# Roots and inverse roots of small tiles: powers on GpSimd in place of ScalarE's root, a Newton step and reciprocals

## The chip, the core and the metric

The kernel runs on one core of one Trainium2 chip. The time is the device time of one execution in microseconds (us). The median of three runs before the change is 863.87 us (863.44 to 865.81). The profile was taken in an execution of 861.47 us, whose span is 859.7 us with a mean granted TensorE clock of 0.921.

The engines are named as in the profile: PE is TensorE (matmuls), PEld its weight load, DVE is VectorE, ACT is ScalarE, POOL is GpSimd, SP only issues transfers.

## What is computed

Four graph layers run on x (3327 nodes, 64 features) and a dense 0/1 adjacency matrix (3327 x 3327). Each layer adds its result to x, and each begins with a layer norm and a relu:

```python
m = mean(x); v = var(x)
h = maximum((x - m) / sqrt(v + eps), 0)
x = x + layer(h, adj, ...)
```

- Layers 0 and 3 are hyperbolic: a weight sigmoid(left_i + right_j) * adj_ij for each pair of nodes, a logarithmic map of node j seen from node i, the weighted sum over j, an exponential map and a projection onto the ball. Norms of rows enter them through `sqrt(sum(x*x))`, tanh and artanh.
- Layer 1 weights the last neighbours of a row by powers of a half ("decay").
- Layer 2 is a GRU pair fed by signed sums over neighbours and a signed attention.

So square roots and inverse roots occur once per node at a few places: in the four norms as 1/sqrt(v + eps), at the start of layers 0 and 3 as the root of the squared norm, and at their ends in the length of the step and in the projection.

## The kernel before

The nodes are padded to 26 tiles of 128, so a quantity with one value a node is a tile of 128 partitions by 26 elements, and X is 128 x 26 x 64. `HALVES` cuts the 26 tiles into two times 13, and much of the work on X is done in two such halves, so that ScalarE and VectorE can work behind one another.

`sqrt_` (L94) takes a small tile and gives its root: ScalarE computes Sqrt (L98), then VectorE does one Newton step, s = (s + x/s)/2, in four instructions: reciprocal (L99), product (L100), sum (L101), half (L102). Where the inverse is wanted, a fifth instruction (L126, L697, L416) takes the reciprocal.

`norm_relu` (L111) runs at the start of each layer: sums (L117), difference (L120), squares on ScalarE (L121), sums of squares (L123), v + eps (L124), then the root, the reciprocal (L126), and max(h, 0) * sd (L128).

`hyperbolic_series` (L308) is layer 0 (r is None) and layer 3. In its setup, x2 (squared norms, L368) gives ia2 (L375), Xr (L379) and the two half-precision parts hi (L380, on ScalarE) and lo (L384); TensorE transposes them (L391), ScalarE and VectorE copy the transposes out to XT and XE (L393, L395), and small matmuls (L401) give the left and right terms. The root of max(x2, 1) (L381, L382) is copied to `root` (L414) and enters z (L416 to L418), by which the terms are multiplied (L422, L428). The main loop then goes over 104 pairs of a column chunk and a row tile: sigmoid on ScalarE (L504), times adjacency on GpSimd (L512), matmuls (L519, L520), a square on ScalarE (L526), two products on VectorE (L530, L531), accumulating matmuls (L537, L545). Its end (L603 on) is a long file of small instructions on 128 x 26 tiles: L639 to L703, with the root of v2 in layer 3 (L656), Tanh (L646 or L658), the root of n2 (L696) and its reciprocal (L697); then the update of X (L710, L711).

`plain_decay` (L1201) is layer 1: masks on VectorE (L1258), counting matmuls (L1265), Exp on ScalarE (L1271), accumulating matmuls (L1282). Its norm is called at L1303. `plain_gat` (L1345) is layer 2: its norm is at L1367, then the sums over neighbours (L1378), reciprocals of the degrees (L1395 to L1397) on VectorE, and the GRU (L1408 on). `ball` (L278) prepares constants of a hyperbolic layer; for layer 3 it takes the root of one value a partition (L302). `gru_weights` (L1180) loads small weights through GpSimd's DMA queue (L1184 to L1196) and adds biases on GpSimd (L1197).

ScalarE holds one table of functions at a time. Sqrt, Exp, and Sigmoid with Tanh need different tables; a load (ACT_TABLE_LOAD) is put by the compiler ahead of an activation that isn't in the loaded table. `table_of` (L105) runs an activation on one element only to have a load happen early.

What sets the order: outside the main loops each engine's instructions are put in order by a planner of the framework, by data dependencies and its own estimate of when operands are ready; instructions of later program text can come early. Inside `tc.manual_schedule` (the main loop of the hyperbolic layers, L442; most of `plain_decay`, L1242) the order on ScalarE, VectorE, TensorE and GpSimd is that of the program text. Each engine works through its queue in order, and an instruction that waits holds up all behind it. In `plain_decay`, GpSimd also adds a bias to all of X (L1333), written at step 4 of the loop.

Of the kernel before, what the change touches and what calls it, by code (L numbers as in the profile page):

```python
# [9 lines left out]
F32 = mybir.dt.float32  # L10
# [3 lines left out]
AF = mybir.ActivationFunctionType  # L14
OP = mybir.AluOpType
# [4 lines left out]
P = 128  # L20
T = 26
# [25 lines left out]
def tile_gnn4(ctx: ExitStack, tc: tile.TileContext, x, adjT, att0, b0, w1, bias1, w_gat, a_gat,  # L47
# [4 lines left out]
    V, G, A, PE = nc.vector, nc.gpsimd, nc.scalar, nc.tensor  # L52

    const = ctx.enter_context(tc.tile_pool(name="const", bufs=1))
# [8 lines left out]
    def column(value, name):  # L63
        t = const.tile([P, 1], F32, name=name)
        V.memset(t, value)
        return t

    one_c = column(1.0, "one_c")
    tiny_c = column(1e-19, "tiny_c")
    spare = const.tile([P, 1], F32, name="spare")  # L70
    nodes = const.tile([P, T], F32, name="nodes")
    V.memset(nodes, 1.0)
# [21 lines left out]
    def sqrt_(pool, src, name):  # L94

        s0 = pool.tile(list(src.shape), F32, name=name)
        rc = pool.tile(list(src.shape), F32, name=name + "_r")
        A.activation(s0, src, AF.Sqrt)  # L98
        V.reciprocal(rc, s0)  # L99
        V.tensor_mul(rc, rc, src)  # L100
        V.tensor_add(s0, s0, rc)  # L101
        V.tensor_scalar(s0, s0, 0.5, None, op0=OP.mult)  # L102
        return s0

    def table_of(f, after=None):  # L105

        A.activation(spare, one_c if after is None else after, f)
# [3 lines left out]
    def norm_relu(pool, h, dst=None):  # L111

        s = pool.tile([P, T], F32, name="ln_s")
        v = pool.tile([P, T], F32, name="ln_v")
        sq = pool.tile([P, T, D], F32, name="ln_sq")
        for ts in HALVES:
            V.reduce_sum(s[:, ts], X[:, ts, :], axis=AX.X)  # L117
        V.tensor_scalar(s, s, 1.0 / D, None, op0=OP.mult)
        for ts in HALVES:
            V.tensor_sub(h[:, ts, :], X[:, ts, :], wide(s[:, ts]))  # L120
            A.activation(sq[:, ts, :], h[:, ts, :], AF.Square)  # L121
        for ts in HALVES:
            V.reduce_sum(v[:, ts], sq[:, ts, :], axis=AX.X)  # L123
        V.tensor_scalar(v, v, 1.0 / D, LN_EPS, op0=OP.mult, op1=OP.add)  # L124
        sd = sqrt_(pool, v, "ln_sd")
        V.reciprocal(sd, sd)  # L126
        for o, ts in enumerate(HALVES):
            V.scalar_tensor_tensor(h[:, ts, :] if dst is None else dst[:, o], h[:, ts, :], 0.0, wide(sd[:, ts]),  # L128
                                   op0=OP.max, op1=OP.mult)
# [148 lines left out]
    def ball(att, b_att, r, min_norm, min_norm2, after=None):  # L278

        k = "0" if r is None else "1"  # L280
        wc = const.tile([P, 2], F32, name="wc" + k)
        with nc.allow_non_contiguous_dma(reason="128 weights"):
            for o in range(2):
                nc.scalar.dma_start(wc[o * D:(o + 1) * D, :],
                                    bass.AP(tensor=att.tensor, offset=att.offset, ap=[[1, D], [D, 2], [1, 1]]))
        wlr = const.tile([P, 2, 3], BF, name="wlr" + k)
        for i in range(3):
            G.tensor_copy(wlr[:, :, i], wc)
            if i < 2:
                G.tensor_tensor(wc, wc, wlr[:, :, i], op=OP.subtract)  # L290
        bcol = const.tile([P, 1], F32, name="bcol" + k)
        nc.scalar.dma_start(bcol, bcast_rows(b_att))
        cc, sqc, isqc, um, maxn2 = [const.tile([P, 1], F32, name=n + k) for n in ("cc", "sqc", "isqc", "um", "maxn")]
        if r is None:
            for t, value in ((cc, 1.0), (sqc, 1.0), (isqc, 1.0), (um, 0.0), (maxn2, min_norm2)):
                V.memset(t, value)
        else:
            nc.scalar.dma_start(cc, bcast_rows(r))
            V.scalar_tensor_tensor(cc, after, -3e38, cc, op0=OP.min, op1=OP.max)
            V.tensor_mul(cc, cc, cc)  # L300
            V.reciprocal(cc, cc)
            V.tensor_copy(sqc, sqrt_(const, cc, "sq"))  # L302
            V.reciprocal(isqc, sqc)
            V.tensor_scalar(um, sqc, min_norm / MIN_NORM, None, op0=OP.mult)
            V.tensor_scalar(maxn2, cc, min_norm2, None, op0=OP.mult)
        return wlr, bcol, cc, sqc, isqc, um, maxn2

    def hyperbolic_series(r, params, ok, masks=None, done=None):  # L308
# [17 lines left out]
        with ExitStack() as st:  # L326
# [14 lines left out]
            root = pers.tile([P, T], F32, name="root")  # L341
            wlr, bcol, cc, sqc, isqc, um, maxn2 = params

            with tc.tile_pool(name="hsp", bufs=1) as tp, tc.tile_pool(name="hsps", bufs=2, space=PSUM) as ps:
                A.memzero(X0)
                Xe = tp.tile([P, T, KE], F16, name="Xe")
                E = Xe[:, :, D:]
# [13 lines left out]

                H = tp.tile([P, T, D], F32, name="H")
                norm_relu(tp, H)
                sq = tp.tile([P, T, D], F32, name="sq")
                for ts in HALVES:
                    A.activation(sq[:, ts, :], H[:, ts, :], AF.Square)
                for ts in HALVES:
# [3 lines left out]
                ax = tp.tile([P, T], F32, name="ax")  # L371
# [6 lines left out]
                for ts in HALVES:  # L378
                    V.tensor_mul(Xr[:, ts, :], H[:, ts, :], wide(ia2[:, ts]))  # L379
                    A.activation(hi[:, ts, :], Xr[:, ts, :], AF.Copy, scale=SX)  # L380
                V.tensor_scalar(root, x2, 1.0, None, op0=OP.max)  # L381
                root_ = sqrt_(tp, root, "zs")  # L382
                for ts in HALVES:
                    V.scalar_tensor_tensor(lo[:, ts, :], Xr[:, ts, :], SX, hi[:, ts, :], op0=OP.mult, op1=OP.subtract)  # L384

# [25 lines left out]
                    V.tensor_copy(E[:, :, k:k + src.shape[-1]], src)  # L411


                V.tensor_copy(root, root_)  # L414
                z = tp.tile([P, T], F32, name="z")
                V.reciprocal(z, root)  # L416
                V.tensor_mul(z, z, ax)
                V.tensor_scalar(z, z, 0.5 * ARTANH_CLIP / SX, isqc, op0=OP.mult, op1=OP.mult)  # L418
                lr = tp.tile([P, T, 2], F32, name="lr")
                V.reduce_sum(lr, pw[:, :6 * T].rearrange("p (t k i) -> p t k i", k=2, i=3), axis=AX.X)  # L420
                left = tp.tile([P, T], F32, name="left")
                V.tensor_mul(left, lr[:, :, 0], z)  # L422
                pl = parts3(left, "pl", BF)
                table_of(AF.Sigmoid, root[:, :1])
                pe = ps.tile([P, 4 * P], F32, name="pe", bufs=1)
                PE.matmul(pe[:3 * T, :P], pl.rearrange("p t k -> p (t k)"), ident_bf, start=True, stop=True)
                A.activation(LT, pe[:3 * T, :P], AF.Copy)
# [175 lines left out]
            with tc.tile_pool(name="hse", bufs=1) as tp:  # L603
# [30 lines left out]
                t = new("t")  # L634
                if r is None:


                    f = MIN_NORM
                    p2 = new("p2")  # L639
                    V.tensor_scalar(p2, v2, f * f, None, op0=OP.mult)  # L640
                    by, g = new("by"), new("g")
                    V.tensor_scalar(by, p2, -1.0, 1.0, op0=OP.mult, op1=OP.add)
                    V.tensor_scalar(g, by, MIN_NORM, None, op0=OP.max)
                    V.reciprocal(g, g)
                    V.tensor_mul(t, root, g)
                    A.activation(th, t, AF.Tanh)  # L646
                    V.reciprocal(t, t)
                    V.tensor_mul(th, th, t)
                    V.tensor_mul(th, th, g)
                    y2 = mul("y2", th, th)  # L650
                    V.tensor_mul(y2, y2, x2)
                    V.scalar_tensor_tensor(vh, vh, f, th, op0=OP.mult, op1=OP.mult)
                else:

                    V.tensor_scalar(t, v2, 1e-8, None, op0=OP.max)
                    t = sqrt_(tp, t, "ts")  # L656
                    V.tensor_scalar(t, t, um, None, op0=OP.max)
                    A.activation(th, t, AF.Tanh)  # L658
                    V.reciprocal(t, t)
                    V.tensor_mul(th, th, t)  # L660
                    y2 = mul("y2", th, th)
                    V.tensor_mul(y2, y2, v2)
                    V.tensor_mul(vh, vh, th)
                    p2 = x2
# [23 lines left out]
                n2 = mul("n2", ah, x2)  # L688
# [4 lines left out]
                V.tensor_mul(mm, mm, am)  # L693
                V.tensor_add(n2, n2, mm)
                V.tensor_scalar(n2, n2, maxn2, None, op0=OP.max)
                n2 = sqrt_(tp, n2, "ns")  # L696
                V.reciprocal(n2, n2)  # L697
                V.tensor_scalar(n2, n2, 1.0 - 0.004, 1.0, op0=OP.mult, op1=OP.min)
                V.tensor_scalar(n2, n2, isqc, None, op0=OP.mult)
                V.tensor_mul(ah, ah, n2)  # L700
# [14 lines left out]
    def hyperbolic(att, b_att, r, min_norm, min_norm2):  # L715
# [7 lines left out]
        with ExitStack() as st:  # L723
# [17 lines left out]
            with tc.tile_pool(name="hyp", bufs=1) as tp, tc.tile_pool(name="hyps", bufs=2, space=PSUM) as ps:  # L741
# [8 lines left out]

                H = tp.tile([P, T, D], F32, name="H")
                norm_relu(tp, H)
                sq = tp.tile([P, T, D], F32, name="sq")
# [447 lines left out]
    def plain_decay(masks, zo, deg):  # L1201
# [10 lines left out]
        with ExitStack() as st:  # L1212
# [29 lines left out]
            with tc.tile_pool(name="pdacc", bufs=1, space=PSUM) as pa, tc.manual_schedule(  # L1242
# [57 lines left out]
                make_mask(1)  # L1300
                with tc.tile_pool(name="pdp", bufs=1) as tp:
                    H = tp.tile([P, T, D], F32, name="H")
                    norm_relu(tp, H)  # L1303
                    table_of(AF.Exp)
                    parts = split2(pers, H, "h2")
                for o in range(2):
                    cnt[o] = pa.tile([P, 2, 512], F32, name=f"cnt{o}")
                for k in range(K_ + 2):
# [29 lines left out]
                    if k - 2 >= T:  # L1338
                        b = steps[k - 2][1]
                        drop_diagonal(masks[b // 2][:, b % 2, :], b, 0, NP)  # L1340
                table_of(AF.Sqrt)
            with tc.tile_pool(name="pdps", bufs=2, space=PSUM) as ps:
                from_pairs(ps, outP, add, wt, range(6, T // 2))

# [195 lines left out]
```

## Time and profile before

The table gives times of the timeline, in us from the span's start.

| stage | stretch |
|---|---|
| layer 0: norm and setup | 5.3 to 33.3 |
| layer 0: main loop | 33.3 to 283.6 |
| layer 0: end | 283.6 to 304.9 |
| layer 1: norm | 304.9 to 320.2 |
| layer 1: loop | 320.2 to 447 |
| layer 2: end of layer 1, norm | 447 to 478.7 |
| layer 2: sums, then GRU | 478.7 to 560 |
| layer 3: norm and setup | 560 to 588 |
| layer 3: main loop | 588 to 831 |
| layer 3: end, store | 831 to 859.7 |

A line of the timeline gives start, duration, engine, line of the kernel, operation, what is written and read, shapes, and in brackets how long the engine had been idle before and what ended that. Several instructions of one line can stand in one row (x2). VectorE overlaps the start of an instruction with the end of the one before when there is no dependency between them, so starts can lie closer together than durations.

In the profile ACT_TABLE_LOAD occurs 12 times, each of 1283 ns: five at L98, four at L107 (inside `table_of`), one each at L345, L658 and L1426. The small Sqrt activations at L98 are ten: four in norms, two in setups, two for n2, one for the step's length in layer 3, one for the constant of one value a partition. Each takes 203 to 226 ns.

### The profile page before, as it was taken

The numbers are of one execution on the slowest core, as the hardware profiler recorded it, in microseconds if no ns is written. First come the engines' busy times: TensorE is split into PE (matmuls) and PEld (weight loads), VectorE is DVE, ScalarE is ACT, GpSimd is POOL, SyncE is SP. The second block draws the span as 40 slices with busy tenths as digits, with TensorE's granted clock in tenths as the row PEclk, the third lists the DMA queues.
The fourth block names the chain that finished last, engine by engine and source line by source line (L and its number), as shares of the span: only waits on it lengthen the run. The fifth ranks groups of instructions, "written<-read, shape, count | busy, mean of one in ns | idle before, by whom it ended". The sixth has DMA issues, their size and how long they took to land.

```text
span 859.7 us, 11940 instructions
## 1 busy us (share of the span) xinstructions
PE 672.2 (78%) x4264; PEld 245.2 (29%) x4264; DVE 728.3 (85%) x1020; ACT 577.1 (67%) x712; POOL 425.7 (50%) x309
## 2 busy tenths in 40 slices
PE   0489998989989219989990997617999899899960
PEld 0312232323322004434440562212222233232220
DVE  7389888889889899998989946795998889888976
ACT  3578878888978237777770306457888789788751
POOL 3289997998989410003110000005777677676730
PEclk9789999999999759999995899957999999999995
DMA  2556666666665428998944530001000000000001
GB/s 41 139 173 194 190 180 172 184 186 184 185 179 148 170 83 302 358 364 308 360 166 169 195 127 1 0 0 23 1 1 10 1 1 10 1 1 1 1 2 43
DMA packets 53877, 104.27 MB, mean 121 GB/s; under 512 B 8016, under 2 KB 30064, under 8 KB 53808
## 3 DMA queue, kind: packets, MB, share of 16 engines
q1 hardware_dynamic: 48704, 103.10, 37.8%
q10 hardware_dynamic: 4656, 0.08, 0.3%
q8 instruction: 35, 0.57, 0.3%
q14 instruction: 34, 0.28, 0.1%
q0 software_dynamic: 448, 0.24, 0.1%
HBM read 100.85 MB, written 0.85 MB: 118 GB/s over the span
## 4 chain that ended last, share of the span: by engine, by line
PE 46%; DVE 35%; ACT 11%; issue 4%; DMA 2%; ACTq 1%; DVEq 0%; SPq 0%; POOL 0%; POOLq 0%
DVE sig L531 11%; DVE L L530 10%; PE cnt L1265 9%; PE acc L537 7%; PE L L519 6%; PE acc L545 6%; ACT y L526 6%; PE acc L1282 5%; PE L L520 5%; PE acc L1378 4%; ACT sig L504 2%; DMA XC<-XT 1%; DVE deg L1397 1%; DVE X L711 1%; PE pt L391 1%
## 5 line engine op out<-in xcount | busy, mean ns | idle before, releaser
L512 POOL TENSOR_TENSOR sig<-mask,sig 128x768 f32<-128x768 fp8e4 (+1 forms) x104 | 174.5, 1679 | 215.7 <-DMA XC<-XT 153.4
L530 DVE SCALAR_TENSOR_TENSOR L<-y,L 128x768 f32<-128x768 f32 (+1 forms) x208 | 213.3, 1025 | 50.0 <-ACT y L526 48.0
L526 ACT ACTIVATE y<-L,shift_c 128x768 f32<-128x768 f32 (+1 forms) x208 | 198.1, 953 | 81.6 <-PE L L520 80.8
L531 DVE TENSOR_TENSOR sig<-L,sig 128x768 f32<-128x768 f32 (+1 forms) x208 | 213.2, 1025 | 21.7
L512 POOL TENSOR_TENSOR sig<-adj,sig 128x768 f32<-128x768 f32 (+1 forms) x104 | 202.6, 1960 | 27.5 <-ACT sig L504 22.4
L504 ACT ACTIVATE sig<-leftB,right 128x768 f32<-128x768 f32 (+1 forms) x208 | 203.7, 980 | 0.0
L537 PE MATMUL acc<-sig,Xr 128*64 128x384 f32 (+1 forms) x832 | 193.0, 542 | 2.1 <-DVE sig L531 2.1
L519 PE MATMUL L<-XC,XT 128*128 128x384 f16 (+1 forms) x416 | 146.5, 352 | 37.8 <-DVE sig L531 27.9
L520 PE MATMUL L<-XF,XE 73*128 73x384 f16 (+1 forms) x416 | 144.7, 348 | 0.0
L1271 ACT ACTIVATE w<-cnt,ebias 128x832 bf16<-128x832 f32 x104 | 93.7, 950 | 30.5 <-PE cnt L1265 30.5
L1178 DVE TENSOR_SCALAR_CACHE_REDUCE same<-adj 128x1664 bf16<-128x1664 f32 x52 | 97.7, 1879 | 3.1 <-DMA adj<-in 3.0
L519 PEld LDWEIGHTS <-XT 128*128 128x128 f16 x416 | 41.1, 99 | 198.1 <-DVE sig L531 154.7
L545 PE MATMUL acc<-sig,X 128*32 128x384 f32 (+1 forms) x832 | 94.2, 525 | 0.0
L1265 PE MATMUL cnt<-mask,after 128*128 128x416 fp8e4 x208 | 54.9, 347 | 23.3 <-DVE mask L1258 20.7
L178 POOL TENSOR_TENSOR mask<-mask,offdiag 128x128 fp8e4<-128x128 fp8e4 x26 | 13.4, 535 | 107.5 <-PE cnt L1265 105.5
L1265 PE MATMUL cnt<-mask,rest 128*128 128x416 fp8e4 x208 | 54.8, 346 | 12.4 <-ACT w L1271 12.4
L537 PEld LDWEIGHTS acc<-sig,Xr 128*64 128x64 f32 x832 | 41.3, 135 | 70.2 <-issue 63.9
L1258 DVE TENSOR_SCALAR mask<-adj 128x1664 fp8e4<-128x1664 f32 x52 | 53.3, 1033 | 1.4 <-DMA adj<-in 1.2
L1282 PE MATMUL acc<-w,h 128*64 128x416 bf16 x416 | 47.1, 349 | 0.0
L520 PEld LDWEIGHTS <-XE 73*128 73x128 f16 x416 | 41.5, 100 | 18.2 <-issue 2.2
L391 PE MATMUL pt<-ident_h,Xp 128*128 128x128 f16 x52 | 5.9, 313 | 41.5 <-DVE Xp L384 41.5
L1378 PE MATMUL acc<-mask,h 128*64 128x416 fp8e4 x416 | 37.9, 344 | 0.3
(295 smaller groups left out, 567.7 us busy)
## 6 DMA issues: line engine op xcount, KB each, us to landing
adj<-in SPq DMA_DIRECT2D x65, 832.0 KB, 6.4
adj<-in SPq DMA_DIRECT2D x78, 384.0 KB, 3.8
adj<-in SPq DMA_DIRECT2D x26, 512.0 KB, 4.7
XC<-XT SPq DMA_DIRECT2D x12, 96.0 KB, 2.6
X<-in SPq DMA_DIRECT2D x1, 832.0 KB, 4.5
out<-X SPq DMA_DIRECT2D x2, 416.0 KB, 2.7
XC<-XT SPq DMA_DIRECT2D x4, 128.0 KB, 5.1
gw<-in POOLq DMA_DIRECT2D x4, 48.0 KB, 6.4
```

Of the source, the lines that this page charges most:

```text
L504: A.activation(sig, leftB[c], AF.Sigmoid, bias=right[:, b:b + 1])
L512: G.tensor_tensor(sig, adj, sig, op=OP.mult)
L519: PE.matmul(L[:, o, :], XT[:, rows], XC[c][:, o, :], start=True, stop=False)
L520: PE.matmul(L[:, o, :], XE[:, rows], XF[c][:, o, :], start=False, stop=True)
L526: A.activation(ys[k], Ls[k], AF.Square, scale=-0.5 / SX ** 2, bias=shift_c)
L530: V.scalar_tensor_tensor(L, y, G3, L, op0=OP.add, op1=OP.mult)
L531: V.tensor_mul(sig, L, sig)
L537: PE.matmul(acc[c][0][o * D:(o + 1) * D, :n], Xr[:, b, :], sigs[k][:, o, :], start=b == 0, stop=b == T - 1)
L545: PE.matmul(acc[c][1][q:q + 32, :n], X0[:, b - 1 + i, :], w[:, o, :], start=b == 1, stop=b == T - 1, tile_position=(0, q))
L1178: V.tensor_scalar(same, adj, 0.0, 0.0, op0=OP.is_equal, op1=OP.add, accum_out=count)
L1265: PE.matmul(cnt[o][:, h, :BK], w, cols(k, o, h), start=w is after and steps[k][1] == T - 1, stop=True, skip_group_check=True)
L1271: A.activation(ws[k][:, o, :, :], cnt[o][:, :, :BK], AF.Exp, scale=-LN2, bias=ebias)
```

## The change

Every call of `sqrt_` on these paths is replaced by GpSimd's `tensor_tensor` with the operation `pow`, whose second operand is a constant 128 x 26 tile filled with 0.5 or -0.5. The inverse root comes out directly, so Newton step and reciprocal go. In the setup of the hyperbolic layers two powers are taken, one for the root (needed at the layer's end) and one for its inverse (needed for z). With Sqrt gone, ScalarE needs only the tables with Sigmoid and Tanh, and with Exp: the calls of `table_of` are moved or changed to match. The aim is to take table loads, hand-overs and small VectorE instructions out of the file of dependent steps, and to use an engine that is idle there.

```diff
@@ -67,6 +67,10 @@
     tiny_c = column(1e-19, "tiny_c")
+    exponents = {}
+    for value in (0.5, -0.5):
+        exponents[value] = const.tile([P, T], F32, name=f"e{len(exponents)}")
+        V.memset(exponents[value], value)
@@ -122,8 +126,8 @@   (norm_relu)
         V.tensor_scalar(v, v, 1.0 / D, LN_EPS, op0=OP.mult, op1=OP.add)
-        sd = sqrt_(pool, v, "ln_sd")
-        V.reciprocal(sd, sd)
+        sd = pool.tile([P, T], F32, name="ln_sd")
+        G.tensor_tensor(sd, v, exponents[-0.5], op=OP.pow)
@@ -299,7 +303,7 @@   (ball)
-            V.tensor_copy(sqc, sqrt_(const, cc, "sq"))
+            G.tensor_tensor(sqc, cc, exponents[0.5][:, :1], op=OP.pow)
@@ -342,6 +346,7 @@   (hyperbolic_series, setup)
+                table_of(AF.Sigmoid)
                 A.memzero(X0)
...
                 V.tensor_scalar(root, x2, 1.0, None, op0=OP.max)
-                root_ = sqrt_(tp, root, "zs")
+                zr = tp.tile([P, T], F32, name="zr")
+                G.tensor_tensor(zr, root, exponents[-0.5], op=OP.pow)
+                G.tensor_tensor(root, root, exponents[0.5], op=OP.pow)
...
-                V.tensor_copy(root, root_)
                 z = tp.tile([P, T], F32, name="z")
-                V.reciprocal(z, root)
-                V.tensor_mul(z, z, ax)
+                V.tensor_mul(z, zr, ax)
...
-                table_of(AF.Sigmoid, root[:, :1])
@@ -653,7 +657,7 @@   (end of layer 3)
                     V.tensor_scalar(t, v2, 1e-8, None, op0=OP.max)
-                    t = sqrt_(tp, t, "ts")
+                    G.tensor_tensor(t, t, exponents[0.5], op=OP.pow)
@@ -693,8 +697,7 @@   (end of layers 0 and 3)
                 V.tensor_scalar(n2, n2, maxn2, None, op0=OP.max)
-                n2 = sqrt_(tp, n2, "ns")
-                V.reciprocal(n2, n2)
+                G.tensor_tensor(n2, n2, exponents[-0.5], op=OP.pow)
@@ -1300,8 +1303,8 @@   (plain_decay)
+                    table_of(AF.Exp)
                     norm_relu(tp, H)
-                    table_of(AF.Exp)
...
-                table_of(AF.Sqrt)
+                table_of(AF.Sigmoid)
```

## The prediction

> **What bounds the kernel now.** I read the engines' shares first, then busy time by stage, then the chain of work that ended last, then the timeline around each root.
>
> ```profile
> PE 672.2 (78%) x4264; PEld 245.2 (29%) x4264; DVE 728.3 (85%) x1020; ACT 577.1 (67%) x712; POOL 425.7 (50%) x309
> ```
>
> No engine is full over the whole span, since the stages differ. Busy time by stage (columns: stretch, length, then PE, PEld, DVE, ACT and POOL busy with counts, granted clock, DMA share, GB/s) shows where the roots lie:
>
> ```profile
> 5.30:33.30 28.00, 8.12 (x95) 7.33 (x95) 22.28 (x65) 17.41 (x26) 5.99 (x17) 0.96 0.09 11
> 33.30:283.60 250.30, 226.10 (x1300) 67.03 (x1304) 213.09 (x220) 197.42 (x233) 217.85 (x136) 0.97 0.64 180
> ...
> 304.90:320.20 15.30, 1.57 (x5) 0.61 (x6) 14.68 (x19) 6.22 (x9) 3.70 (x1) 0.50 0.33 111
> ...
> 447.00:478.70 31.70, 8.00 (x50) 4.76 (x46) 30.44 (x38) 9.19 (x14) 0.00 (x0) 0.62 0.36 135
> ```
>
> In the second row, a big loop, four engines are busy, and the change touches nothing there. In the other three, and in the starts and ends like them (about 150 us together), TensorE is nearly idle and a single file of VectorE instructions, with a few ScalarE steps in it, sets the time. All roots but one lie in such files, so the latency from the operand to the finished root goes into the end one to one. The last root of the kernel, in the timeline:
>
> ```profile
> 835.83 0.18 DVE L655 TENSOR_SCALAR t<-v 128x26 f32<-128x26 f32 x1
> 836.23 1.28 ACT L98 ACT_TABLE_LOAD   x1 [2.80 <-issue]
> 837.52 0.23 ACT L98 ACTIVATE ts<-t 128x26 f32<-128x26 f32 x1
> 837.76 1.28 ACT L658 ACT_TABLE_LOAD   x1
> 837.78 0.32 DVE L99 RECIPROCAL ts_r<-ts 128x26 f32<-128x26 f32 x1 [1.77 <-ACT ts L98]
> ...
> 838.79 0.24 DVE L657 TENSOR_SCALAR ts<-ts,um 128x26 f32<-128x26 f32 x1
> ```
>
> From the operand at 836.01 to its use at 838.79 is 2.78 us: a table load that is waited for, the root, a Newton step in four VectorE instructions. Where the table is already loaded, root, Newton step and reciprocal take about 1.65 us. Next, the root in the norm ahead of the decay stage, which shows something else:
>
> ```profile
> 310.95 1.96 DVE L123 TENSOR_REDUCE ln_v<-ln_sq 128x13 f32<-128x832 f32 x2
> 311.00 3.70 POOL L1333 TENSOR_TENSOR X<-X,bias 128x1664 f32<-128x1664 f32 x1 [8.01 <-DVE H L120]
> 312.94 1.80 DVE L124 TENSOR_SCALAR ln_v<-ln_v 128x26 f32<-128x26 f32 x1
> ...
> 316.39 1.96 DVE L128 SCALAR_TENSOR_TENSOR H<-H,ln_sd 128x832 f32<-128x832 f32 x2
> ```
>
> L124 is an instruction of 0.12 to 0.18 us elsewhere. Here it lasts 1.80 us and ends 0.04 us after GpSimd's L1333: VectorE was shut out while GpSimd ran.
>
> **What the Trainium skill says.** (1) "SBUF — State Buffer", section "Who interferes with whom": GpSimd shares one port pair with VectorE; a VectorE instruction in a 2-port mode, or with two SBUF inputs, and a GpSimd instruction exclude each other for the whole instruction, first come first served. The trace agrees both ways: L124 above, and at 8.00 us a 128x2 cast on GpSimd that takes 0.65 instead of 0.19 us because L120 (two SBUF inputs) is running. (2) "ScalarE: Activation LUTs", section "What ACT_TABLE_LOAD costs": about 1283 ns a load plus a drain; the trace has 1283 ns on every load, 12 of them, and no row for the drain. (3) The same page, "Table sets": the sigmoid set holds tanh; agreed, Tanh at L646 follows the Sigmoid loop with no load. (4) "GPSIMD Engine Reference", section 7: a dependent fp32 chain costs 4 cycles a step. No page prices a power, and no row here shows one.
>
> **The unknown, p, the time of one 128x26 power on GpSimd.** From below: GpSimd's plain TENSOR_TENSOR takes 189 ns on 128x2 and 456 ns on 128x128 (L290, L178), 2.1 ns an element, so 0.24 us on 26. From above: a logarithm and an exponential as one chain of some 35 dependent steps (my guess) at 4 cycles and the page's 1.2 GHz is 117 ns an element, with the 0.19 us about 3.2 us. I take the geometric middle, 0.9 us, and keep both ends. A hand-over adds about 0.1 us beyond p (VectorE to ScalarE and back shows 0.03 each).
>
> **The change part by part** (removed, then added):
>
> 1. Layer 0, start of ScalarE: one more small activation ahead of the memzero, on the chain there (L121 starts late on ScalarE): +0.2. The load of Sqrt at 11.04 was hidden.
> 2. Layer 0 norm: 12.94 to 14.62, 1.68 us, goes; p + 0.1 comes. GpSimd still has casts and subtractions (L288, L290) until 14.20; behind all of them the power would start 1.2 us late, I take half: p - 1.0.
> 3. Layer 0 root (L381): two powers one after the other, from 18.9. They are needed only at L417, but VectorE's L375, L405 and L379 (2-port or two SBUF inputs) stand behind the root and can't run while GpSimd holds the port, except one between the powers. L379 then starts near 19.15 + 2p in place of 19.60: 2p - 0.45. In return the Newton step, a copy and a reciprocal leave VectorE, and the load of Sigmoid with its dummy (1.49 us on ScalarE, 24.97 to 26.46) no longer stands between the copies of XT, for which L401 waits: about -1.0 (0 to -1.4). With 0.1 for the small instructions: 2p - 1.55.
> 4. Layer 0 end (L695 to L698): 294.87 to 296.48, 1.61, goes; p + 0.1 comes. GpSimd's queue here holds DMA issues of the GRU weights, one waiting to 295.13, the last groups on data until 298. If the power is queued behind those it waits up to 4.4 us; I take 1.0: p - 0.5.
> 5. Decay norm: here queues are in program order, so the power stands ahead of L1333. L124 is no longer stalled (313.1), the power ends at 313.2 + p, but then L1333 follows on GpSimd at once and keeps L128, which has two SBUF inputs, out for 3.70 us, or gets between its halves. L128 starts near 316.9 + p in place of 316.39: p + 0.5. Everything behind (L169, L170, the first weights, then a TensorE-bound loop) moves with it.
> 6. Signed-attention norm. The chain here runs wholly on VectorE because reciprocals of 2.7 us were put into each gap of the Newton step:
>
> ```profile
> 464.49 0.12 DVE L124 TENSOR_SCALAR ln_v<-ln_v 128x26 f32<-128x26 f32 x1
> ...
> 465.52 2.69 DVE L1397 RECIPROCAL deg<-deg 128x416 f32<-128x416 f32 x1
> 468.13 0.12 DVE L100 TENSOR_TENSOR ln_sd_r<-ln_sd_r,ln_v 128x26 f32<-128x26 f32 x1
> ...
> 469.12 2.75 DVE L1397 RECIPROCAL deg<-deg 128x416 f32<-128x416 f32 x1
> 471.79 0.26 DVE L126 RECIPROCAL ln_sd<-ln_sd 128x26 f32<-128x26 f32 x1
> ```
>
> L128 follows at 472.19. With one gap in place of five, one reciprocal (2.7 us) covers the power, and the others fall behind L128, where they have until 515 (VectorE idles 10.4 us before L1406). L128 moves to about 468.1, and TensorE's 36 us of L1378, busy without a gap to 514.6, with it: -4.1 (-1.4 if two reciprocals stay, -5.4 if L128 comes before any). p is hidden up to 2.7 us.
> 7. Layer 3 norm: 566.73 to 568.39: p - 1.55. Its table load ends 0.02 us before the root and costs nothing more.
> 8. Layer 3 root: as 3, from 572.93, with L377 between: 2p - 1.6.
> 9. Layer 3 end, ts: 2.78 goes: p - 2.65. Tanh's load was hidden by the Newton step.
> 10. Layer 3 end, n2: 843.21 to 844.84: p - 1.5.
>
> At nothing: two memsets among those before the input lands (5.37); the 128x1 root of the curvature, under L1378; Exp's load, moved ahead into ScalarE's wait; Sigmoid in place of Sqrt after the decay, a load for a load; the load before L1426, hidden by the first gate matmul.
>
> The sum is 10p - 13.7. With p = 0.9: -4.7, so 863.9 - 4.7 = **859.2 us**. It breaks even at p = 1.37.
>
> **The rivals.** *Cheap power*, p = 0.3, near GpSimd's plain rate: -10.7, 853. For it speaks that 26 elements are little; against it, that a power is many steps. *The powers eat what they save*, p about 1.4, or a shorter power with step 6 lost (p = 0.9 without -4.1 gives -0.6): 862 to 866, say 864. For it: ten powers on the path, four through the port lock. *The power becomes the new wait*, p = 2.5: +11.3, 875, **slower than before**; with 3.2, 882. For it: a loop over dependent steps is not overlapped unless somebody unrolled it, and the ends of layers 0 and 3 have nothing to hide it. Against it: in steps 2, 4, 5, 7, 9 and 10 it needs p over 1.5 on average to lose.
>
> **How the numbers follow.** Forecast (856 to 861) 0.36, cheap power 0.19, eaten up 0.14, slower 0.31. Within 0.3% is 861.3 to 866.5, so faster 0.55, same 0.14, slower 0.31. The range goes from p = 0.45 with the GpSimd queue never in the way (-9.2 - 1.6, 853) to p = 2.7 (+13.3, 877); p beyond these on either side I give 2 in 10.
>
> **What the profile after would show.** The TENSOR_TENSOR rows of the powers give p at once: under 1.1 us right, above 1.5 us wrong in sign. Loads of tables: 3 in place of 12. Step 3 and 8: L375 or L379 start when the second power ends. Step 5: L1333 starts at the power's end and L128 at L1333's. Step 6: at most one L1397 between L124 and L128, and L1378 starting near 474.5 less what the stages before gave. Step 4: GpSimd's order, powers before or after the DMA issues. The prediction is wrong if p is wrong by half a microsecond (5 us), if the power doesn't hold the port (a gain of up to 3.6 us more in 3 and 8, and 3.7 in 5), or if VectorE's order in step 6 stays as it is.

## The result, and the profile after

The changed kernel takes 893.95 us (median of four runs, 893.78 to 895.47) where the kernel before took 864.11 beside it: ratio 1.0346, 95% interval 1.0327 to 1.0365, or 30 us **slower**. Measured again later, the pair gave 1.0352 (1.0328 to 1.0375). The forecast was 859.2 us with a range of 853 to 877; the case that came true is the third rival, whose power was set at 2.5 to 3.2 us.

The profiled execution spans 893.7 us. Line numbers from here on are those of the changed kernel, a few lines higher than before (the norm's power is L130, max(h, 0) * sd is L132, z is L422, the bias is added at L1336). First the engines' shares:

```profile
PE 675.9 (76%) x4264; PEld 245.6 (27%) x4264; DVE 721.2 (81%) x971; ACT 567.0 (63%) x695; POOL 476.3 (53%) x321
```

VectorE and ScalarE have lost work (49 and 17 instructions), as intended, and GpSimd has gained 51 us with twelve more instructions. Busy time by stage, of the three quiet stretches that the prediction showed (norm and setup of layer 0, norm of layer 1, norm of layer 2, each between about the same instructions as before, but the second only up to the first Exp, 1.0 us short of the first matmul; columns as there):

```profile
5.30:40.60 35.30, 7.84 (x95) 7.33 (x95) 19.98 (x54) 16.04 (x23) 19.44 (x20) 0.99 0.06 6
321.70:342.20 20.50, 1.54 (x4) 0.58 (x5) 15.74 (x15) 4.87 (x6) 8.13 (x2) 0.50 0.24 83
470.00:499.00 29.00, 8.00 (x48) 4.96 (x44) 22.92 (x26) 9.02 (x15) 4.54 (x1) 0.62 0.41 148
```

The first stretch has grown from 28.0 to 35.3 us while VectorE, which used to fill four fifths of it, is busy for 19.98. The second is 20.5 us long; up to the first Exp it was 14.3 before (304.9 to 319.18). Only the third has shrunk, from 31.7 to 29.0. How long a power takes stands in the table of GpSimd's groups (after the count: busy time, mean ns of one, idle time before):

```profile
L130 POOL TENSOR_TENSOR ln_sd<-ln_v,e 128x26 f32<-128x26 f32 x4 | 18.0, 4509 | 121.8 <-DVE ln_v L128 121.8
L306 POOL TENSOR_TENSOR sqc<-cc,e 128x1 f32<-128x1 f32 x1 | 0.5, 549 | 19.1 <-DVE cc L305 19.1
```

So p, the unknown of the prediction, is **4.5 us**, five times what was taken and 1.4 times the upper bound. From 128x1 to 128x26 it rises by (4490 - 549) / 25 = 158 ns for each further element of a row. The other groups (L388, L389, L660, L700) have means of 4483 to 4494 ns, the same for exponent 0.5 and -0.5.

To see where the time went, the span was cut at instructions that both kernels have: the first square in a main loop, the last product of it, the start of max(h, 0) * sd (of its second half in layer 1, of its first in layers 2 and 3), the first and last Exp of the decay, v + eps. Times are worked out from these instructions' starts in the traces:

| stage | before | after | difference |
|---|---|---|---|
| start to first square of layer 0 | 43.0 | 50.6 | +7.6 |
| main loop of layer 0 | 238.8 | 240.5 | +1.7 |
| end of layer 0, norm of layer 1 | 35.6 | 47.9 | +12.3 |
| from there to the first Exp | 1.9 | 3.3 | +1.4 |
| decay loop | 125.9 | 125.9 | 0 |
| to v + eps of layer 2 | 19.4 | 19.9 | +0.4 |
| layer 2: v + eps to max(h, 0) * sd | 7.7 | 4.8 | -2.9 |
| to v + eps of layer 3 | 94.4 | 95.5 | +1.1 |
| layer 3: v + eps to max(h, 0) * sd | 1.8 | 4.9 | +3.1 |
| from there to the first square of layer 3 | 21.4 | 24.9 | +3.6 |
| main loop of layer 3 | 239.0 | 239.9 | +1.0 |
| end of layer 3, store | 31.0 | 35.7 | +4.8 |

The differences sum to 34.0 us, not 30, since these are two single executions: the one of before (861.47 us) was a quick one, the one of after (895.47) the slowest of its four. The main loops took 239.0 to 240.8 us in all later kernels too, none of which was meant to touch them; a microsecond there is scatter of single executions. The rest lies in the quiet stages, in which the powers stand. The barest case is the length of the step at the end of layer 3, in the timeline:

```profile
865.06 0.18 DVE L659 TENSOR_SCALAR t<-v 128x26 f32<-128x26 f32 x1
865.55 4.48 POOL L660 TENSOR_TENSOR t<-t,e 128x26 f32<-128x26 f32 x1 [10.51 <-DVE t L659]
870.07 0.24 DVE L661 TENSOR_SCALAR t<-t,um 128x26 f32<-128x26 f32 x1 [4.83 <-POOL t L660]
```

VectorE idles for 4.83 us, with the power as the releaser, and nothing else runs. From operand to use it was 2.78 us before, table load included; it is 4.83 now.

The norm ahead of the decay, in the timeline:

```profile
330.00 4.49 POOL L130 TENSOR_TENSOR ln_sd<-ln_v,e 128x26 f32<-128x26 f32 x1 [16.56 <-DVE ln_v L128]
334.46 3.67 POOL L1336 TENSOR_TENSOR X<-X,bias 128x1664 f32<-128x1664 f32 x1
334.52 5.43 DVE L132 SCALAR_TENSOR_TENSOR H<-H,ln_sd 128x832 f32<-128x832 f32 x2 [4.60 <-POOL ln_sd L130]
...
340.90 1.28 ACT L1274 ACT_TABLE_LOAD   x1
```

Two more costs stand behind the power here. L1336 follows it on GpSimd at once (334.46) and has the port before L132 starts (334.52), so two instructions of 1.0 us take 5.43. And a table load, which was hidden before, stands in front of the first Exp: `table_of(AF.Exp)` depends on no data, and the planner had moved it from here to the start of the kernel (8.97 us), where it delayed the first squares instead (10.64 against 9.33). Exp was then replaced by Sigmoid at 41.46 and loaded once more here. There are five loads, not three.

The setup of layer 0, in the timeline:

```profile
22.86 4.49 POOL L388 TENSOR_TENSOR zr<-root,e 128x26 f32<-128x26 f32 x1 [4.35 <-DVE good L439]
27.37 0.19 DVE L422 TENSOR_TENSOR z<-zr,ax 128x26 f32<-128x26 f32 x1 [4.29 <-POOL zr L388]
27.42 4.49 POOL L389 TENSOR_TENSOR root<-root,e 128x26 f32<-128x26 f32 x1
...
27.88 1.95 DVE L384 TENSOR_TENSOR Xr<-H,ia 128x832 f32<-128x832 f32 x2
```

VectorE waits for the first power, but not for the port: L384, with two SBUF inputs, runs at its old 1.95 us in the middle of the second power. What waits is L422, z, which the planner had put *ahead* of L380 and L384 in VectorE's queue; its result isn't needed before the left and right terms at 35.5 us.

The end of layer 0, in the timeline. L699, which makes n2, had started at 303.97:

```profile
308.78 4.51 POOL L700 TENSOR_TENSOR n<-n,e 128x26 f32<-128x26 f32 x1
313.32 0.18 DVE L701 TENSOR_SCALAR n<-n 128x26 f32<-128x26 f32 x1 [9.11 <-POOL n L700]
```

The power is ready to run at 304.2 and starts 4.57 us later, behind DMA issues for the GRU's weights, some of which wait for data themselves; L701 is 9.11 us away from L699 instead of 1.6. The one place that gained is the norm of layer 2:

```profile
487.93 0.11 DVE L128 TENSOR_SCALAR ln_v<-ln_v 128x26 f32<-128x26 f32 x1
488.12 4.54 POOL L130 TENSOR_TENSOR ln_sd<-ln_v,e 128x26 f32<-128x26 f32 x1 [28.92 <-DVE ln_v L128]
492.70 1.96 DVE L132 SCALAR_TENSOR_TENSOR H<-hn,ln_sd 128x832 f32<-128x832 f32 x2 [4.38 <-POOL ln_sd L130]
494.58 2.75 DVE L1400 RECIPROCAL deg<-deg 128x416 f32<-128x416 f32 x1
```

No reciprocal stands between v + eps and L132 any more; VectorE simply waits for the whole power, and even so L132 comes 2.9 us sooner than behind two reciprocals and a Newton step.

### The profile page after: what moved, and what is told of

Read it like the earlier page. It is cut to its first block, busy times and chain, and to the rows that moved or that the text cites. A ratio compares the mean times of both kernels' runs of the same rounds, so it can differ in the third digit from the quotient of the medians.

```text
span 893.7 us, 11896 instructions
## 1 busy us (share of the span) xinstructions
PE 675.9 (76%) x4264; PEld 245.6 (27%) x4264; DVE 721.2 (81%) x971; ACT 567.0 (63%) x695; POOL 476.3 (53%) x321
## 5 line engine op out<-in xcount | busy, mean ns | idle before, releaser
L534 DVE SCALAR_TENSOR_TENSOR L<-y,L 128x768 f32<-128x768 f32 (+1 forms) x208 | 213.3, 1025 | 51.8 <-ACT y L530 49.8
L130 POOL TENSOR_TENSOR ln_sd<-ln_v,e 128x26 f32<-128x26 f32 x4 | 18.0, 4509 | 121.8 <-DVE ln_v L128 121.8
L182 POOL TENSOR_TENSOR mask<-mask,offdiag 128x128 fp8e4<-128x128 fp8e4 x26 | 15.3, 606 | 105.8 <-PE cnt L1268 104.0
```

What stands on the lines that cost most here:

```text
L534: V.scalar_tensor_tensor(L, y, G3, L, op0=OP.add, op1=OP.mult)
```

## The experiments

The theory, A: **the length of one power**, 4.5 us, waited for on the path, makes the loss. Its rivals: the powers shut VectorE out of the port; the loss comes from where the planner put things (z, the table load, the GpSimd queue) and could be had back by placing them better. Times were measured beside the kernel before on three chips, where it took 863.4, 862.5 and 863.8 us; so ratios are what is compared, and stages as in the table above where a difference is small.

| kernel | us | ratio to before (95%) |
|---|---|---|
| changed kernel, again | 893.97 | 1.0352 (1.0328 to 1.0375) |
| cheap operations for the powers | 858.09 | 0.9938 (0.9915 to 0.9961) |
| Exp's table tied to data | 892.87 | 1.0347 (1.0322 to 1.0371) |
| a third power in each setup | 903.36 | 1.0469 (1.0440 to 1.0498) |
| a plain sum in each setup | 891.56 | 1.0339 (1.0308 to 1.0369) |
| inverse root applied late | 886.25 | 1.0282 (1.0259 to 1.0304) |
| GRU weights issued by SyncE | 890.52 | 1.0335 (1.0312 to 1.0358) |
| bias added later | 890.78 | 1.0334 (1.0311 to 1.0358) |
| the last four mends together | 878.12 | 1.0157 (1.0132 to 1.0182) |
| kernel before, one power in layer 2 | 861.12 | 0.9984 (0.9969 to 0.9999) |
| kernel before, powers where hidden | 859.83 | 0.9952 (0.9935 to 0.9970) |

"The last four mends" are Exp's table and the three rows directly above that one.

**1. The powers made cheap.** Every power becomes a sum or product of the same shapes on GpSimd (the norm's, shown here for layers 1 and 2, is a sum in layers 0 and 3); everything else is the changed kernel. The roots are left out of the computation.

```diff
-        G.tensor_tensor(sd, v, exponents[-0.5], op=OP.pow)
+        G.tensor_tensor(sd, v, exponents[0.5], op=OP.mult)
...
-                G.tensor_tensor(zr, root, exponents[-0.5], op=OP.pow)
-                G.tensor_tensor(root, root, exponents[0.5], op=OP.pow)
+                G.tensor_tensor(zr, root, exponents[-0.5], op=OP.add)
+                G.tensor_tensor(root, root, exponents[0.5], op=OP.add)
```

> The changed kernel with every power replaced by a plain GpSimd instruction of the same shape and place in the queues (an add, in the plain layers a product); so this kernel leaves the roots out. Theory A, the length of the power: nine powers stand in the way of the end (one each in the four norms, one of the two in each hyperbolic setup, three at the ends); each falls from 4.49 us to about 0.25, so 894.0 - 9 x 4.24 = 856, faster than before by about 8. Rival B, the moved work (GpSimd's queue, the port shared with VectorE, the loads of tables): the time stays well above before, 870 or more. Half of each would be about 875.

858.09 us, some 35.5 under the changed kernel (35.9 from the medians, 35.2 from the ratios). The replacements take 0.24 us each (L131 at 14.13, L703 at 841.60), so each exposed power had cost about 4.25, and 35.5 is between eight and nine of these. The stages say nine: the start -8.7, end and norm -8.5, layer 2 -4.3, layer 3's norm -4.2, its setup -3.6, its end -8.3. So, with everything placed as in the changed kernel, the length of the power is more than the whole loss, and all the rest of the change together, with powers at almost nothing, is worth 0.6%. A holds, as long as the powers stand where they stand; whether better places would hide them is asked in experiments 3 to 5.

**2. Does a power hold the port?** The first kernel adds a third 128x26 power to each setup, whose result nobody reads; the second a plain sum over 128x1664, of no use either.

```diff
                 G.tensor_tensor(root, root, exponents[0.5], op=OP.pow)
+                extra = tp.tile([P, T], F32, name="extra")
+                G.tensor_tensor(extra, x2, exponents[0.5], op=OP.pow)
```

> The changed kernel with a third power of 128x26 behind the two in each hyperbolic setup, its result not used. If a power holds the port shared with VectorE as long as it lasts, VectorE's two-input and 2-port instructions wait 4.5 us more in each setup: up to 903. If it doesn't hold it, nothing waits for it and the time stays at 894.0 within 0.5.

```diff
                 G.tensor_tensor(root, root, exponents[0.5], op=OP.pow)
+                G.tensor_tensor(sq, sq, sq, op=OP.add)
```

> The changed kernel with a plain GpSimd add over 128x1664 (3.7 us, result not used) behind the two powers in each hyperbolic setup, the counterpart of the third power. A plain add holds the shared port, as in the decay stage: VectorE stands still up to 3.7 us in each setup, 897 to 901. If neither kind holds it, 894.0 within 0.5 in both.

The third power cost 9.4 us (10.6 by the ratios), about two powers, which taken alone would speak for the port. The timeline of this kernel's layer 0 tells otherwise (line numbers in each timeline are those of its own kernel; L441 here was L439):

```profile
22.84 4.49 POOL L391 TENSOR_TENSOR extra<-x,e 128x26 f32<-128x26 f32 x1 [4.06 <-DVE x L373]
22.89 0.23 DVE L386 TENSOR_SCALAR root<-x 128x26 f32<-128x26 f32 x1
23.04 0.17 DVE L441 SCALAR_TENSOR_TENSOR good<-x,nodes 128x26 f32<-128x26 f32 x1
27.30 4.48 POOL L388 TENSOR_TENSOR zr<-root,e 128x26 f32<-128x26 f32 x1
31.81 0.19 DVE L424 TENSOR_TENSOR z<-zr,ax 128x26 f32<-128x26 f32 x1 [8.37 <-POOL zr L388]
```

L386 and L441 (two inputs) start inside the extra power and take 0.23 and 0.17 us (0.17 and 0.18 in the changed kernel). The extra power only went *first* in GpSimd's queue, so the one that z waits for came 4.5 us later, twice in the kernel. The plain sum at the same spot:

```profile
22.90 2.96 POOL L390 TENSOR_TENSOR sq<-sq 128x1664 f32<-128x1664 f32 x1 [4.05 <-DVE x L373]
22.95 2.95 DVE L386 TENSOR_SCALAR root<-x 128x26 f32<-128x26 f32 x1
```

The same L386 now lasts 2.95 us and ends with the sum: this one does hold it. The port theory falls for the power and stands for the sum. The total, 891.56 us, was expected in neither case (897 to 901, or 894.0): the planner here placed z behind Xr and lo (L384 at 26.46, z at 30.49), both powers ran under them, and 5.9 us of added work on GpSimd left the time where it was (1.0339 against 1.0346), about what hiding the powers gave back.

**3. z out of the way.** If z's place is what costs, then taking the inverse root out of z and multiplying it in at the end of the setup should give the power back.

```diff
-                V.tensor_mul(z, zr, ax)
-                V.tensor_scalar(z, z, 0.5 * ARTANH_CLIP / SX, isqc, op0=OP.mult, op1=OP.mult)
+                V.tensor_scalar(z, ax, 0.5 * ARTANH_CLIP / SX, isqc, op0=OP.mult, op1=OP.mult)
...
+                V.tensor_mul(left, left, zr)
...
+                V.tensor_mul(right, right, zr)
```

> The changed kernel, but the inverse root is used only after the small matmuls (left and right are multiplied by it there), so that no VectorE instruction ahead of Xr waits for GpSimd. The last two runs showed that a power leaves VectorE's port free and that z, waiting in VectorE's queue, is what holds Xr back. If that is the whole cost of the setup, both powers are hidden there: 4.4 us less in each hyperbolic setup, 894.0 - 8.8 = 885. If the powers hold VectorE in any other way, over 890.

886.25 us. The start is 45.7 us long in place of 49.8 to 50.6, the setup of layer 3 21.4 in place of 24.9: 4.1 to 4.9 and 3.5 us, about one power each. L384 starts at 23.48, with powers running from 22.94 to 31.98, and takes its 1.95 us:

```profile
22.94 4.49 POOL L388 TENSOR_TENSOR zr<-root,e 128x26 f32<-128x26 f32 x1 [4.35 <-DVE good L440]
23.48 1.95 DVE L384 TENSOR_TENSOR Xr<-H,ia 128x832 f32<-128x832 f32 x2
27.50 4.48 POOL L389 TENSOR_TENSOR root<-root,e 128x26 f32<-128x26 f32 x1
```

Confirmed: the two powers of each setup are hidden whole.

**4. The other placements, one at a time.** Exp's table kept in its place by reading X; the GRU weights' transfers issued from SyncE's queue; the bias addition tied to step 4 of the loop, where it is written, by a copy of the bias that ScalarE makes there (GpSimd, with nothing ahead of it, had run it early).

```diff
-                    table_of(AF.Exp)
+                    table_of(AF.Exp, X[:, 0, :1])
```

> The changed kernel with the early activation for Exp's table reading a column of X as layer 0 leaves it, so that it can't come at the kernel's start. Theory A with a second term for tables: three loads in place of five; the start of layer 0 is 1.3 us shorter (the load of Exp stood ahead of the squares on ScalarE) and the decay stage's start 1.3 us shorter (the load at the first weights was waited for), so about 891.3 (-2.6); the load ahead of the first sigmoid is hidden. Rival B, tables explain a large part: 885 or less. If tables cost nothing: 894.0.

```diff
-            nc.gpsimd.dma_start(wg[o:o + D, :], w_gat)
+            nc.sync.dma_start(wg[o:o + D, :], w_gat)
...
-                nc.gpsimd.dma_start(bt[q, :3], bi)
+                nc.sync.dma_start(bt[q, :3], bi)
```

> The changed kernel with the small GRU weights loaded through SyncE's queue instead of GpSimd's. In the changed kernel the power at layer 0's end was ready to start at 304.2 us and started at 308.8, behind thirteen transfer issues of GpSimd. If that wait is what it cost, 894.0 - 4.5 = 889.5. If the power waits for something else, 894.

```diff
+            bias2 = pers.tile([P, D], F32, name="bias2")
...
-                        G.tensor_tensor(X, X, bias[:, None, :].to_broadcast([P, T, D]), op=OP.add)
+                        A.activation(bias2, bias, AF.Copy)
+                        G.tensor_tensor(X, X, bias2[:, None, :].to_broadcast([P, T, D]), op=OP.add)
```

> The changed kernel with the bias add of layer 1 held back to the loop (it reads a copy of the bias that ScalarE makes at the loop's fourth step), so that it doesn't follow the power at once. If the 3.7 us that the relu of layer 1 waits for the shared port are on the path, and the loop has room for the add: 890.3. If the loop has no room, the masks there wait as long: 894. If the port wait was not on the path: 894 as well, but with the relu's first half starting at the power's end and the masks undisturbed.

Each did in its stage what it was made for, but for the start in the Exp edit. Exp: to the first Exp 1.9 in place of 3.3 us. At the start the squares again begin at 9.36, but v + eps done earlier doesn't help, as the power still starts at 14.13 behind GpSimd's casts; the 1.3 us there are not had. Queue: end and norm 43.3 in place of 47.9; the power starts at 302.89, 0.3 after L699. Bias: 44.4 in place of 47.9, since L132 takes 1.96 us again. But the bias now meets a mask in the loop:

```profile
350.00 3.70 POOL L1338 TENSOR_TENSOR X<-X,bias 128x1664 f32<-128x1664 f32 x1 [17.18 <-ACT bias L1337]
350.43 5.09 DVE L1262 TENSOR_SCALAR mask<-adj 128x1664 fp8e4<-128x1664 f32 x2
```

Two masks of 1.02 us take 5.09, and the decay loop is 128.4 us long in place of 125.9. Of the 3.5 us gained in the norm 2.5 are lost again: most of the port wait was moved rather than saved. The ratios (1.0347, 1.0335, 1.0334) differ from the changed kernel's 1.0346 and 1.0352 by less than their intervals; the stages carry these findings, not the times.

**5. The four mends together.**

> The changed kernel itself, beside the next two on one chip: 894 us, ratio 1.034 to 1.036 to the kernel before, as on record. It is there so that the four mended waits of the next kernel can be counted against it.

> The changed kernel with all four placements mended that were tried one at a time: the inverse root applied late in the setups, the GRU weights' transfers issued by SyncE, Exp's table tied to the data, the bias added four steps later. Alone they were worth 8.9, 5.3, about 1 and 4.5 us of span. Theory A (the length of one power, exposed six times, is what is left): they add up, 893.9 - 19.7 = about 874.5 us, still 10 slower than before, since the norms of layers 0, 1 and 3, the step's length and the two projections each still wait a whole power of 4.49 us where root, Newton step and reciprocal took 1.6 to 2.8 (six times 4.6 less 11.1 = +16, less 6 for the setups, layer 2 and loads that pay). Rival B (queue order is the real cost, the power's length is hidden once its place is right): at or below 864 us.

878.12 us, 15.9 under the changed kernel beside it, of 19.7 expected. By stage against that run: start -3.8, end and norm -8.0, first Exp -1.4, decay loop +1.9, layer 3's setup -3.0; that is 14.3, and 14.1 in the span. The expectation had added spans of single executions, which scatter by some 2 us; by stage the mends do add up. What stays is 1.6% over the kernel before, and VectorE still waits for whole powers, at the end of layer 0 and in the norm of layer 1:

```profile
302.81 0.18 DVE L702 TENSOR_SCALAR n<-n 128x26 f32<-128x26 f32 x1 [4.59 <-POOL n L701]
324.01 1.96 DVE L132 SCALAR_TENSOR_TENSOR H<-H,ln_sd 128x832 f32<-128x832 f32 x2 [4.59 <-POOL ln_sd L130]
```

So it does in the norms of layers 0 and 3 and twice in layer 3's end. So half of the loss could be had back by placing: 6.8 of the 14.3 us by hiding the powers of the setups, 4.6 by the queue (as much as alone), the remainder by the bias and the table. The other half is powers with nothing to hide them. The rival that placement is all falls, as far as these four placements go.

One wait of these kernels stays open. In the setup of layer 3 ScalarE's copies of the transposes came 0.86 us apart here, and with the Exp and the queue edits, instead of 0.5 to 0.6; TensorE's granted clock was 0.50 over these 11 us, 0.72 in the changed kernel and 0.80 before. With the Exp and the queue edits, which touch nothing there, the stage took 26.4 us each in place of 24.9, some 1.4 more. Why the clock was granted differently wasn't tried.

**6. A power only where it pays.** The kernel before with the power in layer 2's norm alone, and then a version that takes powers only in layer 2, in both setups with the inverse root applied late, and for the one value a partition. Sigmoid's table is to be loaded behind the norm, and Sqrt's early for the end of layer 3. In the edit, `power=True` makes this norm alone take the power.

```diff
-                norm_relu(tp, tp.tile([P, T, D], F32, name="hn"), H.rearrange("p k o d -> p o k d"))
+                norm_relu(tp, tp.tile([P, T, D], F32, name="hn"), H.rearrange("p k o d -> p o k d"), power=True)
```

> The kernel before with the power in the norm of layer 2 alone; root, Newton step and reciprocals everywhere else. In the changed kernel the way from v to H was 4.65 us there in place of 7.58, since two of three reciprocals fell behind H. If this carries to the end alone: 863.9 - 2.9 = 861.0, faster than before by 0.3%. If it is given back by the end of layer 2, or if the gain needs the other powers: 863.9.

> The kernel before with powers only where other work covers them: both setups with the inverse root applied late, the norm of layer 2, the one value a partition; root, Newton step and reciprocal stay everywhere else. Sigmoid's table is then loaded behind the norm, out of the way of the transposes' copies, and Sqrt's for the ends of the layers early. Theory A (a power costs nothing where 4.5 us of independent work lie beside it): layer 2 gives 1.4 as measured alone, the two setups 1.3 to 2 us each, so about 859 us where the kernel before takes 863, ratio 0.995. Rival (GpSimd's powers delay others even when hidden): 862 us or more, ratio 0.999 to 1.003.

Layer 2 alone: from v + eps to max(h, 0) * sd 4.8 in place of 7.7 us, of which the time shows 1.4 (0.9984). Where the remainder goes isn't settled; the stretch up to layer 3's norm is 0.6 longer. All of it: 859.83 us, ratio 0.9952, 0.5% **faster than the kernel before** and the sum that was expected.

The stages don't bear out the parts. Layer 2 gives -2.9, though its power isn't covered: VectorE waits 4.4 us for it, as in the changed kernel. The setups, of which 1.3 to 2 us each were expected, give -0.6 (the start) and +0.7 (layer 3's, again at a clock of 0.50). The 0.6 may be due to the table as well as to the powers, since the load of Sigmoid no longer stands between the copies of the transposes; the tables weren't moved without the powers. The early load of Sqrt missed its place: the planner put it into the main loop of layer 3 (679.29), where Sigmoid's table had to be loaded again (681.59), and the root of the step's length still waits for a load of its own (836.63). So there are 13 loads, one more than before.

So two powers in a setup, 4.5 us each, cost nothing clear where other work lay beside them, while one of them had cost its whole length when it was waited for. This fits A. That the powers of the setups gain anything isn't shown, and where the 4.1 us (by the ratio) come from stays open: of this kernel the slowest of six executions was profiled (861.71 us) and of the kernel before a quick one (861.47), so that their spans are alike (859.8 and 859.7) and the stages can't add up to a gain.

## Why the prediction was wrong

**The step that failed is "the unknown, p".** It was bounded at 0.24 to 3.2 us and taken at 0.9; the rows show 4.5. The lower bound came from GpSimd's plain sums; the upper was my guess of 35 dependent steps for one logarithm and exponential, priced by the Trainium skill ("GPSIMD Engine Reference", section 7) at 4 cycles a step: an estimate of 117 ns an element, where 158 were measured. A count of steps that nobody had shown couldn't be a bound, and the geometric middle of a range of one to thirteen gave the low end a weight that nothing in the profile supported. The prediction's own sum, 10p - 13.7, gives +31.2 us with p = 4.49, 895 us. That is near the 893.95 measured, though partly by luck, since terms were off in both directions:

| steps | by the sum, p = 4.49 | by stage |
|---|---|---|
| 1, 2: start and norm of layer 0 | +3.7 | +3.9 |
| 3: setup of layer 0 | +7.4 | +3.7 |
| 4: end of layer 0 | +4.0 | +7.5 |
| 5: norm of layer 1 | +5.0 | +4.8 |
| table of Exp | 0 | +1.4 |
| 6: norm of layer 2 | -4.1, or -2.3 with p beyond 2.7 | -2.9 |
| 7: norm of layer 3 | +2.9 | +3.1 |
| 8: setup of layer 3 | +7.4 | +3.6 |
| 9, 10: end of layer 3 | +4.8 | +4.8 |

- Steps 2, 5, 7, 9 and 10 were right but for p. In step 5 the order foretold, power, then L1336, then L132, is what the timeline shows.
- Steps 3 and 8 named the wrong wait. They had both powers hold the port, on the Trainium skill ("SBUF — State Buffer", section "Who interferes with whom"), which speaks, for VectorE instructions with two SBUF inputs, of any GpSimd instruction that reads SBUF. The third power and the plain sum show that it holds for a sum and not for a power; the measurement decides. What did wait was z in VectorE's queue, which was said to be needed only at L417; the planner's order wasn't in the trace of before, and the case that z comes first wasn't weighed. One power each was paid in place of two.
- Step 4 took 1.0 us for GpSimd's queue out of a range up to 4.4. It was 4.57, shown by the queue edit.
- Step 6 took one reciprocal to cover the power. None did, and the whole power stands on VectorE as idle time; the gain comes from the reciprocals that no longer stand in the gaps.
- "Exp's load at nothing" failed: an instruction that depends on nothing has no place of its own, and the planner moved it.
- With powers at 0.24 us the sum gives -11.3; the first experiment gave -5.3. So the fixed part was too hopeful by 6 us. By stage 3.3 of it lie in steps 4 and 5, where a cheap power too stood 4.64 us in GpSimd's queue, 1.4 in Exp's table and 1.1 in step 8; step 6 on the other hand gave 7.2 in place of 4.1. What is left lies in stretches that the change doesn't touch.
- One reading was off without touching the sum: v + eps (L124) isn't 0.12 to 0.18 us everywhere else. In layer 0 of the kernel before it lasts 0.70 us, from 12.24 to 12.94, beside a GpSimd instruction that ends at 12.87.

## What to carry to other kernels

An operation that no row prices is best measured by itself before it is put on a path ten times; if it can't be, its upper bound has to be one that something shows, and the likeliest time shouldn't be drawn towards the rate of simpler operations. Before work is moved to an idle engine, ask how much other work lies beside the new operation: here the powers of the setups could be hidden under VectorE's work, and those with nothing beside them each cost more than the chain that they replaced. The one stage that got shorter, the norm of layer 2, did so because two reciprocals left its path, not because its power was hidden. After such a move look at two queues, for what stands ahead of the moved instruction on its new engine, and for where its first reader stands on the old one.

## What the runs showed of the hardware

- A float power with a tensor as exponent takes GpSimd 0.55 us on 128x1 and 4.48 to 4.58 us on 128x26, some 158 ns for each further element of a row, with 0.5 and -0.5 alike. A sum or product of 128x26 takes 0.24 us, and a sum of 128x1664 2.96 us.
- During a power VectorE's instructions with two SBUF inputs run undisturbed (L384, 1.95 us for two halves; L441, 0.17). During a plain sum a small VectorE instruction lasted as long as the sum (2.95 us instead of 0.17).
- TensorE's granted clock in one and the same stage, the setup of layer 3, was 0.80 before, and 0.72, 0.66 or 0.50 in later kernels. With the same instructions in it, it took 26.4 us at 0.50 and 24.9 at 0.72. That the clock is what made it longer, and why it was granted differently, wasn't tried.
